# Gathers and sums of the routed experts as two lines of the planned order, six tiles of gathered rows, and a new test for shared chunks

## Chip, core and metric

One Trainium2 chip, one core. The metric is the device time of one execution in microseconds (us). The kernel before has a median of 2207.93 us in three runs (2204.1, 2207.93, 2208.98).

## What is computed

Input is x, two sequences of 2048 tokens with 256 features, all in float32. Four residual blocks follow one another:

```python
x = x + attention(layernorm(x))   # 16 heads, causal, weights scaled by a spectral norm
x = x + ffn(layernorm(x))         # f = 0: 8 experts, top 2 of them, plus a shared expert
x = x + gated(layernorm(x))       # x * softplus(x W1 + b1) * (x W2 + b2 . x W3 + b3)
x = x + ffn(layernorm(x))         # f = 1: same weights as f = 0
```

where ffn is

```python
scores = softmax(xt @ gate_w.T + gate_b); top_w, top_i = top_k(scores, 2)
out_e  = (silu(xt @ w1[e].T + b1[e]) * (xt @ w3[e].T + b3[e])) @ w2[e].T + b2[e]
y      = sum over the two picked experts of top_w * out_e
z      = (silu(xt @ ws1.T + bs1) * (xt @ ws3.T + bs3)) @ ws2.T + bs2
return y + z
```

## The kernel before, in words

The 4096 tokens are eight chunks of 512 (TC = 8), four to each of the two batches b; a chunk has four blocks of 128 tokens (NB = 4). X[c] holds a chunk in SBUF from start to end, and every stage adds to it in place.

The first half is the attention, with an order written out in a loop (L546 and after). The change touches only where three of its small tiles live: part (L318), nmt (L362) and rc (L425).

The second half, from about 1143 us, runs the two ffn blocks and the gated block. Its parts are Python generators. Each yield is a tuple of costs (DVE, ACT, PE, POOL) in us of what is issued next; a yield of None means "can't go on yet".

- route(f, c) (L736) normalizes a chunk, flips it to a feature-major tile xT and picks two experts for each token. sort(f, b) (L797) gives each token its slots in a list ordered by expert; weigh (L865) gives the gates. These three are the line routing.
- scatter(f, b) (L884) writes the normalized rows of a batch to the DRAM list XS[b] by 32 indirect DMAs from POOL, each followed by a small memset, and then marks (f, b) as placed.
- routed(f, b) (L1039) is the expert block, 39 blocks of 128 slots (EB): load rows of XS (SP queue), turn them (PE, ACT), up (PE; ea on DVE; Silu on ACT; es on DVE), turn, down (PE; ey on DVE), write to YS[b] (SP queue). When it is done, (f, b) is marked as ran.
- shared(f, c) (L1000) is the shared expert on one chunk: eight steps of the matmul s, then four of sy, 1.72 us of PE each. It reads the chunk's xT and frees it at the eighth step.
- combine(f, c) (L908) gathers, for each block, its two rows per token from YS[b] by two indirect DMAs from POOL into tiles yg (four of them), and adds them to X[c] by two DVE instructions (the sums, L933). For f = 1 it then issues the chunk's store to the output on SP.
- mixer(c) (L946) is the gated block on a chunk, after its combine: norm (with pow on POOL, L717), flip, z (PE, DVE), softplus through ACT, DVE and POOL (POOL lines L976, L986, L990), and the add to X[c] (L994).

moving() (L1156) is one line: scatter (0,0), scatter (0,1), then combine of the four f = 0 chunks of batch 0, scatter (1,0), combine of those of batch 1, scatter (1,1), and combine of all f = 1 chunks. mixing() is the line of the eight mixers, routing() the third. The three are in sides, in this order.

The planner writes the program. The main loop (L1214) takes steps of the expert block and of a shared chunk in turn ("mains"); free[2] is PE's planned time, called now here. After each step beside() (L1178) issues what fits from the sides: it goes through them in order, issues the first step that may go, and starts again. A step may go if each engine that it uses is planned free no later than now + LEAD (DVE 1.7, ACT 1.3, POOL 2.7), and its line's own time no later than now + AHEAD (DVE 1.5, ACT 1.5, POOL 2.7). A line's time is the planned end of its last step plus 0.2. A shared chunk is begun if its xT is there and either all three xT tiles are live (live[0] >= XTS), or no expert block is running or placed; the last condition is "not wait".

So the order on each engine is fixed when the program is built; on the chip only semaphores act. The names (0,1) and the like below are (f, b) for scatters and experts and (f, c) for shared chunks.

Of the kernel before, what the change touches and what calls it, by code (L numbers as in the profile page):

```python
# [8 lines left out]
F32 = mybir.dt.float32  # L9
# [7 lines left out]
P = 128  # L17
D = 256
# [26 lines left out]
KTE = 8  # L45
EARLY = 8
LOW = -3e38
LAG = 3


@with_exitstack
def hybrid_block(
# [87 lines left out]
    with tc.tile_pool(name="aw", bufs=1) as aw, ExitStack() as aw_ctx:  # L140
# [104 lines left out]
            yield 1  # L245

        with ExitStack() as ac:
            xnp = ac.enter_context(tc.tile_pool(name="xnp", bufs=1))
            xtp = ac.enter_context(tc.tile_pool(name="xtp", bufs=3))
            skp = ac.enter_context(tc.tile_pool(name="skp", bufs=2))  # L250
# [62 lines left out]
            class Maxima:  # L313


                def __init__(self, b, c, g):
                    self.unit, self.q = (b, c, g), qT[b, g, c]
                    self.part = small.tile(  # L318
                        [P, NB, 4, NCH], F32, tag="part", name=f"part_{b}_{g}_{c}"
                    )  # L320
                    self.full = [(kc, i) for kc in range(c) for i in range(NB)] + [(c, NB - 1)]
                    self.diag = [(c, i) for i in reversed(range(NB - 1))]
                    self.left = len(self.full) + len(self.diag)
# [33 lines left out]
            def shift(b, c, g, part, t):  # L357

                nc.vector.tensor_reduce(
                    t[:, :, 0:4], part[:, :, :, 0:c + 1], AX.X, ALU.max, negate=True  # L360
                )
                tt = small.tile([P, NB * 32], F32, tag="nmt", name=f"nmt_{b}_{g}_{c}", bufs=2)  # L362
                nc.vector.transpose(tt, t.rearrange("p n r -> p (n r)"))
                rows = qT[b, g, c][HD::32, :].rearrange("j (n a t) -> j n a t", a=4, t=32)
                for a in range(4):
                    nc.sync.dma_start(
                        rows[:, :, a, :],
                        tt[32 * a:32 * a + 4, :].rearrange("j (n t) -> j n t", t=32),
                    )
# [48 lines left out]
            def finish(b, c, g):  # L418

                ot = acc.pop((b, c, g))  # L420
                ps = bank(f"pso_{b}_{g}_{c}")
                for i in range(NB):
                    nc.tensor.transpose(ps[:, i * P:(i + 1) * P], ot[:, i * P:(i + 1) * P], ident)
                pv = ps.rearrange("p (m r) -> p m r", r=32)
                rc = small.tile([P, NB * 4], F32, tag="rc", name=f"rc_{b}_{g}_{c}")  # L425
                nc.vector.reciprocal(rc, pv[:, :, HD])
                if g == 0:
                    otok[b, c] = okp.tile([P, NB, NG, 4 * HD], F32, tag="otok", name=f"otok_{b}_{c}")
                nc.vector.tensor_tensor(
                    otok[b, c][:, :, g, :].rearrange("p n (j d) -> p n j d", d=HD),  # L430
                    pv[:, :, 0:HD].rearrange("p (n j) d -> p n j d", j=4),
                    rc.rearrange("p (n j) -> p n j", j=4).unsqueeze(3).to_broadcast([P, NB, 4, HD]),
                    ALU.mult,
                )
# [249 lines left out]

    scores, picks, sel, slots, gates, words = {}, {}, {}, {}, {}, {}
    xhat, xhatT = {}, {}
    live, held = [0], [0]

    added, mixed, sorted_, placed, joined, ran = set(), set(), set(), set(), set(), set()
# [2 lines left out]
    def feature_major(nm):  # L692
        while live[0] >= XTS:
            yield None
        live[0] += 1
        return cw.tile([P, 2, CH], F32, tag="xT", name=f"xT_{nm}", bufs=XTS)

    def token_major(nm):
# [37 lines left out]
    def route(f, c):  # L736

        b, q = divmod(c, NCH)
        nm = f"{f}_{c}"
        while f == 1 and c not in mixed:  # L740
            yield None
        if q == 0:
            scores[f, b] = rw.tile([P, BLK, E], F32, tag="lg", name=f"lg_{f}_{b}", bufs=1)
            picks[f, b] = rw.tile([P, TOPK, BLK, E], F32, tag="pick", name=f"pick_{f}_{b}", bufs=1)
            sel[f, b] = rw.tile([P, E, BLK], BF16, tag="sel", name=f"sel_{f}_{b}", bufs=1)
        blk = slice(q * NB, (q + 1) * NB)
        xn = yield from token_major(f"f{nm}")
        yield from normed(X[c], xn, f"f{nm}")
        xhat[f, c] = xn
        yield (0, 0, 0, 2.4)  # L750
        nc.gpsimd.tensor_tensor(
            X[c], X[c], bs2_s.unsqueeze(1).to_broadcast([P, NB, D]), ALU.add
        )
        xT = yield from feature_major(f"f{nm}")
        yield from flipped(xn, xT, f"f{nm}")
        xhatT[f, c] = xT
        yield (0.2, 0, 1.8, 0)
        ps = side_bank(f"psl_{nm}")
        for i in range(NB):
            for d in range(2):  # L760
                nc.tensor.matmul(  # L761
                    ps[:, i * E:(i + 1) * E], xT[:, d, i * P:(i + 1) * P], gw_s[:, d, :],
                    start=d == 0, stop=d == 1,
                )
        lg = scores[f, b][:, blk, :]
        nc.vector.tensor_tensor(
            lg, ps[:, :NB * E].rearrange("p (n e) -> p n e", e=E),
            gb_s.unsqueeze(1).to_broadcast([P, NB, E]), ALU.add,
        )
        yield (1.6, 0, 0, 0)  # L770

        ge = small.tile([P, NB, E, E], F32, tag="ge", name=f"ge_{nm}", bufs=2)
        nc.vector.tensor_tensor(
            ge, lg.unsqueeze(2).to_broadcast([P, NB, E, E]),
            lg.unsqueeze(3).to_broadcast([P, NB, E, E]), ALU.is_ge,
        )
        nc.vector.tensor_tensor(
            ge, ge, before.unsqueeze(1).to_broadcast([P, NB, E, E]), ALU.mult
        )
        up = small.tile([P, NB, E], F32, tag="rup", name=f"rup_{nm}", bufs=2)  # L780
        dn = small.tile([P, NB, E], F32, tag="rdn", name=f"rdn_{nm}", bufs=2)
        nc.vector.reduce_sum(up, ge, axis=AX.X)
        nc.vector.reduce_sum(dn, ge.rearrange("p n e j -> p n j e"), axis=AX.X)
        yield (0.6, 0, 0, 0)
        nc.vector.tensor_tensor(up, up, dn, ALU.subtract)
        pk = picks[f, b]
        for k in range(TOPK):
            nc.vector.tensor_tensor(
                pk[:, k, blk, :], up, level[:, k, :].unsqueeze(1).to_broadcast([P, NB, E]),
                ALU.is_equal,  # L790
            )
        nc.vector.tensor_tensor(
            sel[f, b][:, :, blk].rearrange("p e n -> p n e"), pk[:, 0, blk, :], pk[:, 1, blk, :],
            ALU.add,
        )
# [109 lines left out]
        yield (0, 0, 0, 0.5)  # L905
        placed.add((f, b))

    def combine(f, c):  # L908

        b, q = divmod(c, NCH)  # L910
        while (f, b) not in ran:
            yield None
        got = {}
        for i in range(NB + 1):
            if i < NB:
                n = q * NB + i
                for k in range(TOPK):
                    yield (0, 0, 0, 1.3)
                    y = ew.tile([P, D], F32, tag="yg", name=f"yg_{f}_{c}_{i}_{k}", bufs=4)
                    nc.gpsimd.indirect_dma_start(  # L920
                        out=y, out_offset=None, in_=YS[b],
                        in_offset=bass.IndirectOffsetOnAxis(
                            ap=slots[f, b][:, k, n:n + 1], axis=0
                        ),
                    )
                    got[i, k] = y
            elif q == NCH - 1:
                yield (0, 0, 0, 1.5)
            if i > 0:
                yield (1.0, 0, 0, 0)  # L930
                n = q * NB + i - 1
                for k in range(TOPK):
                    nc.vector.scalar_tensor_tensor(  # L933
                        X[c][:, i - 1, :], got.pop((i - 1, k)), gates[f, b][:, k, n:n + 1],
                        X[c][:, i - 1, :], ALU.mult, ALU.add,
                    )
        if f == 0:
            joined.add(c)
            return
        while (f, c) not in added:  # L940
            yield None
        nc.sync.dma_start(
            out[c * CH:(c + 1) * CH, :].rearrange("(n p) d -> p n d", p=P), X[c]
        )
# [211 lines left out]
    def moving():  # L1156
        yield from scatter(0, 0)
        yield from scatter(0, 1)
        for f, b in rows[:2]:
            for c in chunks(b):  # L1160
                yield from combine(f, c)
            yield from scatter(1, b)
        for c in range(TC):
            yield from combine(1, c)

    def mixing():
        for c in range(TC):
# [5 lines left out]
    LEAD = (1.7, 1.3, 0.0, 2.7)  # L1173
    AHEAD = (1.5, 1.5, 0.2, 2.7)

    sides = [[0.0, g, None] for g in (moving(), mixing(), routing())]

    def beside():  # L1178

# [34 lines left out]
    while sides or todo or shares or mains:  # L1214
        if "share" not in mains:
            fit = [s for s in shares if s in xhatT]
            wait = "experts" in mains or (todo and todo[0] in placed)
            if fit and (live[0] >= XTS or not wait):
                shares.remove(fit[0])
                mains["share"] = shared(*fit[0])  # L1220
        if "experts" not in mains and todo and todo[0] in placed:
# [88 lines left out]
```

## Time and profile before

| | us |
|---|---|
| median of the runs (three) | 2207.93 |
| lowest and highest | 2204.1, 2208.98 |
| the profiled execution | 2117.58 |
| its span, first to last instruction | 2115.8 |
| mean granted TensorE clock in it | 0.983 |
| PE busy | 2010.0 (95%) |
| DVE busy | 1386.0 (66%) |
| POOL busy | 870.5 (41%) |
| 128 gathers (L920) busy on POOL | 128.2 |
| 128 sums (L933) busy on DVE | 66.5 |

The profile is of one execution, whose own time lies 90 us below the median of the timed runs; all durations below are from it. PE is TensorE's matmuls, DVE VectorE, ACT ScalarE, POOL GpSimd, SP the queue that issues the direct DMAs. In a row of the order of time the columns are start, duration, engine, line, instruction, output and input with shape, count, and in brackets the idle time before it and what ended it. In the stage table each engine has its busy time and number of instructions, and PEclk is the granted TensorE clock.

Events of the second half, from the orders of time of PE and POOL: experts (0,0) end at 1424; gathers of the f = 0 chunks of batch 0 issue from 1427.2 to 1494.5; scatter (1,0) 1638.8 to 1679.7; gathers of batch 1's f = 0 chunks 1680.0 to 1751.1; scatter (1,1) 1890.4 to 1930.7; gathers of the f = 1 chunks of batch 0 1931.0 to 1998.9; experts (1,1) end at 2062.5; gathers of the f = 1 chunks of batch 1 2065.9 to 2108.6.

### The profile page before, as it was taken

The page shows a single profiled execution, that of the slowest core. Times are in us where ns is not written, and L with a number is a line of the kernel's source. Part 1 is how long each engine was busy: PE and PEld are TensorE (multiplying, and loading weights), DVE is VectorE, ACT ScalarE, POOL GpSimd, SP SyncE. Part 2 cuts the span into 40 slices and gives each one's busy share as a digit, 9 for nine tenths or more (in the row PEclk, how much of TensorE's full clock was granted, in tenths as well). Part 3 has the DMA queues.
Part 4 walks back from the last instruction along what each step waited for, and adds up shares of the span by engine and source line. Part 5 has one row for each costly group of instructions (what it writes and reads, how often), then busy time and mean ns, then how long its engine had stood idle before and what let it go on. Part 6 is the DMA issues. An engine that isn't in the chain of part 4 may idle for free.

```text
span 2115.8 us, 36162 instructions
## 1 busy us (share of the span) xinstructions
PE 2010.0 (95%) x11840; PEld 1087.9 (51%) x11840; DVE 1386.0 (66%) x3428; ACT 1075.5 (51%) x1566; POOL 870.5 (41%) x1153
## 2 busy tenths in 40 slices
PE   6999999999999999999998999999999999999993
PEld 3444444444445444444444666655656556655662
DVE  4777777787776777777851546446776378663643
ACT  1657577577776667767784122324433244431330
POOL 4334345254343343434454171605422753346305
PEclk8999999999999999999999999999999999999997
DMA  3212110000000000000002321423210332013523
GB/s 97 77 36 64 34 33 5 10 1 7 6 7 6 6 1 7 4 4 4 2 2 86 135 90 46 150 80 113 80 41 18 130 112 78 28 40 134 165 76 121
DMA packets 87604, 113.04 MB, mean 53 GB/s; under 512 B 16385, under 2 KB 75137, under 8 KB 87297
## 3 DMA queue, kind: packets, MB, share of 16 engines
q1 hardware_dynamic: 73488, 75.08, 11.1%
q0 software_dynamic: 12288, 33.57, 4.8%
q8 instruction: 101, 1.65, 0.3%
q10 hardware_dynamic: 1648, 2.10, 0.3%
q14 instruction: 79, 0.64, 0.1%
HBM read 54.59 MB, written 51.64 MB: 50 GB/s over the span
## 4 chain that ended last, share of the span: by engine, by line
PE 82%; DVE 7%; ACT 3%; issue 3%; POOL 3%; DMA 2%; DVEq 0%; SPq 0%; POOLq 0%; ACTq 0%
PE st L386 15%; PE o L405 13%; PE psm L341 13%; PE eu L1085 10%; PE s L1011 7%; PE ed L1109 5%; PE sy L1028 4%; PE psk L275 3%; PE tr L1070 3%; PE psz L961 1%; PE psj L454 1%; POOL xs L893 1%; PE psv L301 1%; DVE junk L350 1%; PE psl L761 1%
## 5 line engine op out<-in xcount | busy, mean ns | idle before, releaser
L390 ACT ACTIVATE pt<-st 128x1024 f32<-128x1024 f32 (+3 forms) x640 | 556.0, 895 | 176.1 <-PE psm L341 123.3
L341 PE MATMUL psm<-kT,qT 32*128 32x512 f32 (+3 forms) x2560 | 621.8, 565 | 10.7 <-DMA kT<-sk 4.4
L386 PE MATMUL st<-qT,kT 32*128 32x512 f32 (+3 forms) x2560 | 604.8, 553 | 1.3 <-ACT pt L390 1.3
L355 DVE TENSOR_REDUCE part<-psm 128x1 f32<-128x512 f32 x768 | 477.1, 681 | 117.1 <-PE psm L341 113.6
L416 POOL TENSOR_TENSOR oa<-oa,op 128x512 f32<-128x512 f32 (+3 forms) x288 | 313.8, 1090 | 450.5 <-ACT op L414 450.0
L386 PEld LDWEIGHTS st<-qT,kT 32*128 32x128 f32 x2560 | 264.4, 184 | 228.0 <-ACT pt L390 140.5
L341 PEld LDWEIGHTS psm<-kT,qT 32*128 32x128 f32 x2560 | 274.6, 184 | 76.0 <-issue 20.1
L350 DVE CUSTOM_DVE_ANT_0 junk<-psm,maskq 128x384 bf16<-128x384 f32 (+3 forms) x512 | 250.8, 490 | 94.8 <-PE psm L341 29.9
L405 PE MATMUL o<-pt,v 128*32 128x512 f32 (+3 forms) x2560 | 301.2, 541 | 11.2 <-DVE part L355 6.7
L1085 PE MATMUL eu<-we,turned 128*128 x560 | 263.7, 593 | 0.0
L1092 ACT ACTIVATE es<-ea 128x256 f32<-128x256 f32 x156 | 65.0, 417 | 353.9 <-DVE ea L1090 353.8
L1011 PE MATMUL s<-xT_f,ws 128*128 128x512 f32 x512 | 232.6, 598 | 0.0
L920 POOL DMA_INDIRECT yg<-ys,slot x128 | 128.2, 1001 | 233.2 <-issue 84.6
L414 ACT COPY op<-o 128x512 f32<-128x512 f32 (+3 forms) x288 | 148.6, 516 | 64.5 <-PE o L405 46.9
L1090 DVE TENSOR_TENSOR ea<-eu,be 128x512 f32<-128x512 f32 x156 | 107.4, 689 | 109.5 <-PE eu L1085 108.9
L1109 PE MATMUL ed<-we,turned 128*128 x624 | 162.7, 383 | 14.5 <-ACT turned L1075 14.5
L393 POOL TENSOR_SCALAR_AFFINE_SELECT pt<-pt 128x256 f32<-128x256 f32 x256 | 103.0, 409 | 176.9 <-ACT pt L390 173.0
L405 PEld LDWEIGHTS o<-pt,v 128*32 128x32 f32 x2560 | 52.2, 108 | 214.4 <-DVE part L355 124.4
L1109 PEld LDWEIGHTS ed<-we,turned 128*128 128x128 f32 x624 | 116.1, 190 | 88.0 <-issue 49.0
L893 POOL DMA_INDIRECT xs<-xn_f,slot x128 | 124.9, 975 | 86.3 <-DVE slot L847 59.3
L1011 PEld LDWEIGHTS s<-xT_f,ws 128*128 128x128 f32 x512 | 95.3, 192 | 102.7 <-issue 96.4
L1085 PEld LDWEIGHTS eu<-we,turned 128*128 128x128 f32 x560 | 97.6, 190 | 75.1 <-issue 72.9
(268 smaller groups left out, 2099.4 us busy)
## 6 DMA issues: line engine op xcount, KB each, us to landing
xs<-xs SPq DMA_DIRECT2D x156, 128.0 KB
ys<-ey SPq DMA_DIRECT2D x156, 128.0 KB
xs<-zeros SPq DMA_DIRECT2D x78, 128.0 KB
we<-in_we_dram SPq DMA_DIRECT2D x8, 768.0 KB
kT<-sk SPq DMA_DIRECT2D x128, 32.0 KB
out_dram<-x SPq DMA_DIRECT2D x8, 512.0 KB
x<-in_x_dram SPq DMA_DIRECT2D x6, 512.0 KB
be<-in_be_dram SPq DMA_DIRECT2D x1, 3072.0 KB
```

What stands on the lines that cost most here:

```text
L341: nc.tensor.matmul(ps[:, :n], self.q[r, i * P:(i + 1) * P], kT[b, g, kc][r, :n], start=True, stop=True,)
L350: nc.vector.tensor_tensor_reduce(junk[:, :n], ps[:, :n], maskq[:, CH - n:], 1.0, LOW, ALU.add, ALU.max, m,)
L355: nc.vector.reduce_max(m, ps[:, :n], axis=AX.X)
L386: nc.tensor.matmul(st[:, i, off:], k[r, ks], q[r, off:], start=True, stop=True)
L390: nc.scalar.activation(pt[:, :, off:], st[:, :, off:], AF.Exp)
L405: nc.tensor.matmul(o[32 * j:32 * j + 32, off:], V[kb // NB][:, kb % NB, 4 * g + j, :], pts[j // 2][:, j % 2, off:], start=True, stop=True,)
L414: nc.scalar.copy(t[:, off:], o[:, off:])
L416: nc.gpsimd.tensor_tensor(a[:, off:], a[:, off:], t[:, off:], ALU.add)
L893: ins = nc.gpsimd.indirect_dma_start(out=XS[b], out_offset=bass.IndirectOffsetOnAxis(ap=slots[f, b][:, k, n:n + 1], axis=0), in_=xhat[f, b ...
L1011: nc.tensor.matmul(ps, w[:, d, cs], xT[:, d, :], start=d == 0, stop=d == 1)
L1085: nc.tensor.matmul(ps, t[:, 1, d * P:(d + 1) * P], we_s[:, bass.ds(v + d * CH, CH)], start=d == 0, stop=d == 1,)
L1109: nc.tensor.matmul(ps[:, 0:D], t[:, 0, d * P:(d + 1) * P], we_s[:, bass.ds(v + 2 * CH + d * D, D)], start=d == 0, stop=d == 1,)
```

## The change

combine is split. gather(f, c) issues the indirect DMAs and puts each block's pair of tiles into a list, landing, of at most GB = 3 blocks; yg has six tiles. combine(f, c) issues the sums, and may place those of a block once the next block's gathers have been issued (counted in sent). moving() now holds the scatters and gathers; a new line combining(), second in sides, holds the sums and stores. A count, turns, holds how many feature-major tiles are still to be asked for (24 in all: 8 by mixers, 16 by routes); the rule for shared chunks "all three xT tiles are live" is now "all three are live and more are to come". To make room, part, nmt and rc of the attention move from the pool small, which stays, to a pool asm that is released with the attention, and the tile ge of route has one buffer, not two.

```diff
+GB = 3
...
+            asm = ac.enter_context(tc.tile_pool(name="asm", bufs=3))
...
-        ge = small.tile([P, NB, E, E], F32, tag="ge", name=f"ge_{nm}", bufs=2)
+        ge = small.tile([P, NB, E, E], F32, tag="ge", name=f"ge_{nm}", bufs=1)
...
+    turns = [TC + 2 * TC]
...
         live[0] += 1
+        turns[0] -= 1
...
-    def combine(f, c):
+    landing = []
+    sent = [0]
+
+    def gather(f, c):
 
         b, q = divmod(c, NCH)
         while (f, b) not in ran:
             yield None
...
+        for i in range(NB):
+            n = q * NB + i
+            rows = []
+            for k in range(TOPK):
+                while len(landing) == GB:
+                    yield None
+                yield (0, 0, 0, 1.3)
+                y = ew.tile([P, D], F32, tag="yg", name=f"yg_{f}_{c}_{i}_{k}", bufs=2 * GB)
+                nc.gpsimd.indirect_dma_start(
...
+                rows.append(y)
+            landing.append(rows)
+            sent[0] += 1
+        if q == NCH - 1:
+            yield (0, 0, 0, 1.5)
+            sent[0] += 1
+
+    def combine(f, c):
+
+        b, q = divmod(c, NCH)
+        for i in range(NB):
+
+            at = (f * TC + c) * NB + i + f * B + b + 2
+            while sent[0] < at:
+                yield None
+            yield (1.0, 0, 0, 0)
+            n = q * NB + i
+            for k, y in enumerate(landing.pop(0)):
+                nc.vector.scalar_tensor_tensor(
+                    X[c][:, i, :], y, gates[f, b][:, k, n:n + 1], X[c][:, i, :],
+                    ALU.mult, ALU.add,
+                )
...
             for c in chunks(b):
-                yield from combine(f, c)
+                yield from gather(f, c)
             yield from scatter(1, b)
         for c in range(TC):
-            yield from combine(1, c)
+            yield from gather(1, c)
+
+    def combining():
+        for f in range(2):
+            for c in range(TC):
+                yield from combine(f, c)
...
-    sides = [[0.0, g, None] for g in (moving(), mixing(), routing())]
+    sides = [[0.0, g, None] for g in (moving(), combining(), mixing(), routing())]
...
-            if fit and (live[0] >= XTS or not wait):
+            if fit and (live[0] >= XTS and turns[0] or not wait):
```

More of the change, by code (lines that the diff above doesn't have):

```diff
@@ L317, in __init__ @@
                     self.unit, self.q = (b, c, g), qT[b, g, c]
-                    self.part = small.tile(
+                    self.part = asm.tile(
                         [P, NB, 4, NCH], F32, tag="part", name=f"part_{b}_{g}_{c}"
@@ L361, in shift @@
                 )
-                tt = small.tile([P, NB * 32], F32, tag="nmt", name=f"nmt_{b}_{g}_{c}", bufs=2)
+                tt = asm.tile([P, NB * 32], F32, tag="nmt", name=f"nmt_{b}_{g}_{c}", bufs=2)
                 nc.vector.transpose(tt, t.rearrange("p n r -> p (n r)"))
@@ L424, in finish @@
                 pv = ps.rearrange("p (m r) -> p m r", r=32)
-                rc = small.tile([P, NB * 4], F32, tag="rc", name=f"rc_{b}_{g}_{c}")
+                rc = asm.tile([P, NB * 4], F32, tag="rc", name=f"rc_{b}_{g}_{c}")
                 nc.vector.reciprocal(rc, pv[:, :, HD])
@@ L912, in combine @@
             yield None
[L913 to L936, printed above, removed]
+        for i in range(NB):
[7 more added lines that the diff above has]
+                nc.gpsimd.indirect_dma_start(
+                    out=y, out_offset=None, in_=YS[b],
+                    in_offset=bass.IndirectOffsetOnAxis(
+                        ap=slots[f, b][:, k, n:n + 1], axis=0
+                    ),
+                )
[17 more added lines that the diff above has]
+                    ALU.mult, ALU.add,
+                )
         if f == 0:
```

## The prediction

> **What bounds the kernel now.** I read the 40 slices first, then the busy times of the last stages, then POOL and PE in order of time, the view of the gathered tile, and the waits.
>
> ```profile
> ## 2 busy tenths in 40 slices
> PE   6999999999999999999998999999999999999993
> ...
> POOL 4334345254343343434454171605422753346305
> ```
>
> PE is full nearly to the end of both halves. The second half starts near 1143 us; what is left of PE's idle time lies in the last slice. The stages show how the end is made:
>
> ```profile
> core 0: us, PE busy (x) PEld busy (x) DVE busy (x) ACT busy (x) POOL busy (x), PEclk, DMA share, GB/s
> ...
> 1950.00:2000.00 50.00, 50.00 (x200) 31.63 (x199) 32.93 (x71) 16.62 (x34) 22.69 (x23) 1.00 0.58 176
> 2000.00:2050.00 50.00, 50.00 (x200) 31.54 (x199) 25.68 (x54) 16.93 (x34) 0.00 (x0) 1.00 0.31 98
> 2050.00:2116.00 66.00, 31.80 (x109) 19.23 (x108) 25.05 (x50) 6.07 (x12) 30.89 (x32) 0.77 0.35 108
> ```
>
> From 2000 to 2050 POOL does nothing: the 32 gathers of the last four chunks need the last expert block. PE in order of time, around that block's end:
>
> ```profile
> 2061.57 1.13 PE L1109 MATMUL ed<-we,turned 128*128 x4 [0.52 <-ACT turned L1075]
> 2062.54 13.90 PE L1011 MATMUL s<-xT_f,ws 128*128 128x512 f32 x32
> 2076.28 7.07 PE L1028 MATMUL sy<-ws,hsh 128*128 128x256 f32 x32
> ```
>
> After it one shared chunk runs, 2062.5 to 2083.4 (20.8 us), and PE is done. POOL gathers from 2065.94 to 2109.6 and the span ends at 2115.8. So the end is the last expert block's end (2062.5) plus 53.3 us, and only one of 16 shared chunks lies in that tail, which has room for more than two. **The end falls if PE reaches 2062.5 earlier: by less idle time before it, or by a whole shared chunk moved behind it.**
>
> PE between experts (1,0) and (1,1):
>
> ```profile
> 1915.03 1.03 PE L1109 MATMUL ed<-we,turned 128*128 x4
> 1915.90 13.90 PE L1011 MATMUL s<-xT_f,ws 128*128 128x512 f32 x32
> 1929.63 1.89 PE L1028 MATMUL sy<-ws,hsh 128*128 128x256 f32 x8
> 1934.29 0.41 PE L1070 MATMUL tr_-4_17532<-ident,xs 128*128 128x128 f32 x2 [2.77 <-DMA xs<-xs]
> ```
>
> When the planner saw (1,1) placed, shared chunk (1,6) had done its eight first steps (13.9 us) and stood before its last four. A chunk once started is interleaved with the experts and ends before them. So a placing earlier by less than about 13 us moves no chunk; by 13 to 34 us it moves one, 20.8 us.
>
> What sets the placing is a chain: gathers and sums, four mixers, routes, sort, scatter. The pow (L717) of mixers 0 to 3 marks its pace:
>
> ```profile
> 1448.82 1.05 POOL L717 TENSOR_TENSOR lnrs_b<-lnve_b,nhalf 128x4 f32<-128x4 f32 x1 [1.53 <-DVE lnve_b L715]
> 1505.97 1.16 POOL L717 TENSOR_TENSOR lnrs_b<-lnve_b,nhalf 128x4 f32<-128x4 f32 x1 [10.54 <-DVE lnve_b L715]
> ...
> 1544.97 1.14 POOL L717 TENSOR_TENSOR lnrs_b<-lnve_b,nhalf 128x4 f32<-128x4 f32 x1 [7.44 <-DVE lnve_b L715]
> ...
> 1581.68 1.04 POOL L717 TENSOR_TENSOR lnrs_b<-lnve_b,nhalf 128x4 f32<-128x4 f32 x1 [6.78 <-DVE lnve_b L715]
> ```
>
> 57, 39, 37 us: the mixer beside the gathers is 19 us slower than its fellows. In batch 1 POOL's order of time gives 54, 42, 38 (1699.9, 1753.9, 1795.9, 1834.0): 16 us. So 35 us is the most that a faster gather stage can give to the chain.
>
> **Two lines instead of one.** By the planner's costs a block is now 2 x (1.3 + 0.2) + 1.0 + 0.2 = 4.2 us, 16 blocks 67 us; the trace agrees (first to last gather issue 1427.2 to 1494.5). Split, the gather line takes 3.0, the sums follow at the same pace: 48 us. On the chip a gather takes 1.25 us (tail), so POOL can follow. Six tiles let it run three blocks ahead. In the tile's view, "who waited for it", POOL stands 74.3 us for its tiles:
>
> ```profile
> L920 POOL DMA_INDIRECT yg<-ys,slot x128: 942/952/1942, 1427.2 to 2108.6; - x128
> ...
>   POOL yg L920: 74.3, 43
>   DVE x L933: 17.4, 21
> ```
>
> None of the 74.3 is worth its size: except in the tail, only what hastens the mixers counts. Nothing but order moves: the same 128 gathers, 128 sums and 8 stores. The gathers move past the mixers' elementwise work on POOL; the stores past nothing on SP that is waited for.
>
> What the split costs: the gather line stands first and refills POOL to its lead of 2.7 us; a mixer's POOL step (pow, L976, L986, L990) then fits only where that lead lies in the last 0.2 us before the next gather. Following the costs by hand from the end of experts (0,0), chunk 0 is joined about 2 us sooner, the pow comes about 12 us later than now (34 after the start, not 22), but the gathers end near 1475, nothing stands before L976 and after, and mixer 0 ends near 1493 instead of 1498.9. Mixer 1's statistics, now held to 1502.8 by the last sums, then start near 1494: 9 us gained. Bounds: 19 (all of the slowdown), and -12 (the pow shut out until 1475, then the 35 us that a free mixer needs from there, 1510). In batch 1 the phase is kinder to the pow; mixer 4 ends 2 us earlier, and the 6 us that sums take from mixer 5 (statistics to flip 8 us, against 4 for mixer 2) go: 8 us, bounds 16 and -14. Sum 17 us, between -26 and 35. I take 17, nearest to the trace's shape, in which the stage ends with its gathers. 17 is beyond 13, so chunk (1,6) goes to the tail.
>
> **Sums earlier in DVE's order.** A sum is placed once the next block's gathers are in the program, no longer when they are planned to end, so DVE, which is in order, may stand before it for data; behind it wait ea, es and ey, and PE waits for those through turned. Landing takes 2.7 to 2.8 us from issue; at the starts of the two stages PE itself waits for xs, so I take 0 to 1.5 us there. DVE's own load rises: per block of 3.02 us, ea 0.69, es 0.42 and ey 0.42, plus 0.99 of sums, 2.5 us or 83%, and the mixer's norm on top. Now PE idles 0 us in 1430 to 1500 and 4 us in 1720 to 1750. I add 3 us, bounds 0 and 10.
>
> The rule that speaks against this: the Trainium skill, SBUF — State Buffer, Who interferes with whom, says that a VectorE instruction with two SBUF inputs contends with a GpSimd one that reads SBUF, and that one blocks fully. A sum has two, yg and x. If gathers counted as such, packing sums beside them could hold each of 64 blocks up to 0.95 us, some 30 us in the two inner stages, on an engine at 83%. The row: in the tail, beside back-to-back gathers, the sums take 0.48 us, as elsewhere; beside L990 one took 3.1 us. So the rule holds for the mixers' POOL work, not for gathers; the split parts sums from that work, and I add nothing.
>
> **Tail.** Twelve gathers from 2065.94 took 18.8 us where 12 x 1.25 is 15.0: 3.8 us lost to sums queued behind the shared chunk's DVE steps. With three blocks of lead this goes when one chunk is in the tail. With two (41.6 us), sums paced at 3.0 hold the gathers part of the way: I give 2.3 of the 3.8 back.
>
> **Shared chunks kept.** The new test matters only while three feature-major tiles are live and none is to come: after the last flip (about 1875) it holds (1,5) back from 1888 until experts (1,0) end. PE then does the same work in another order; the gap before the placing takes (1,5) anyway. 0 us, hidden by that gap; only if the placing came 34 us earlier would it keep three. A little more DVE load in the last sort is at most 2 us of the 17.
>
> **asm, ge.** The first half's three small tiles go to a pool that is released; same instructions. ge with one buffer is written and read by DVE alone: nothing waits. A shift of addresses could change which late tile the first loads wait for: 0, bounds -2 and 3.
>
> **Sum.** 2115.8 - 20.8 (chunk moved) - 1.5 (tail) + 3 (DVE) = 2096.5, that is -19. The profiled execution took 2117.58, the median of the runs is 2207.93, 90 us more; no row shows where, and the saving is of program order, so I carry it over: 2189.
>
> **Rivals.**
> - Chain faster, but by less than 13 us: no chunk moves. -3.8 + 2 to 3: about -1.5, 2206. For it: 17 stands only 4 above the threshold, and jitter of a planner step is 1.7. Against: both stages point the same way.
> - Starved mixers, slower: if the pow is shut out in both stages the placing is late by over 6.9 us, the four steps (1,6) has left, and (1,7) is started before it. Then nothing is left for the tail: +20.8 - 3.8 + 1 = +18, 2226. The point is the phase of the gather line: lead above 2.7 after each step. Against it: the lead drifts by 0.02 us per block and opens the window within about ten blocks.
> - DVE as the bound of the two stages: +10 instead of +3 and no chunk: +6, 2214.
> - The placing comes 34 us early: two chunks more, -40, 2168.
>
> **Chances.** One chunk moved 0.53; none, small gain 0.24; slower by starving or DVE 0.20; two chunks 0.03. A difference of 0.2% (4.4 us) is about what a measurement of this kernel can tell from none. Faster: 0.53 + 0.03 and 0.01 of the second case, 0.57; same 0.23; slower 0.20. The range runs from 2178 (one chunk with the idle time saved too) to 2222, which takes in the unmoved case and most of the slower ones.
>
> **What would show it.** Right: gathers of (0,0) to (0,3) issued within 50 us; L717 of mixers 0 and 1 under 50 us apart; the last expert block near 2044 with 64 matmuls of s behind it, 32 now; "POOL yg" waiting for x under 30 us. Wrong: 32 or none behind it; sums with a long wait for yg inside an expert block; PE waiting for turned by over 10 us more than the 13.2 now.

## The result, and the profile after

After takes 2227.5 us (2222.7 to 2230.2, five runs), before 2207.4 (2201.2 to 2209.0) on the same chip: ratio 1.0096, 95% interval 1.0083 to 1.0109. That is 20 us slower, where 19 us faster was forecast.

One thing must be known to read the rest. The runs were made in six sets, each on one chip, and the sets fall into two kinds: in four of them before took 2199 to 2207 us, in two 2119 to 2120. The profile that the prediction was read from (2117.6 us) is of the second kind, the timed runs shown with it (2207.9) are of the first. I call the chips *disturbed* and *quiet*; one chip was met in two sets, both times disturbed, so that it is the chip and not the hour is likely but not shown. Every ratio below is against before on the same chip. Times of two disturbed chips are set beside each other only for after and for the runs of before again, the new test alone and the four tiles, where before took 2207.4 and 2206.9.

The order came out as forecast. PE in order of time at the end of after (disturbed chip):

```profile
2169.82 1.13 PE L1128 MATMUL ed<-we,turned 128*128 x4 [0.52 <-ACT turned L1094]
2170.78 13.90 PE L1030 MATMUL s<-xT_f,ws 128*128 128x512 f32 x32
2184.52 7.07 PE L1047 MATMUL sy<-ws,hsh 128*128 128x256 f32 x32
2191.42 13.90 PE L1030 MATMUL s<-xT_f,ws 128*128 128x512 f32 x32
```

Two shared chunks stand behind the last expert block, where before had one. But that block ends at 2170.8, not near 2044. The 40 slices of after's page show where the time went:

```profile
PE   7999999999999999999989895979996899958997
...
POOL 4434345254344443344442624034336243353205
```

The first line is PE, the second POOL, in tenths. PE is no longer full in the second half. The stretches with 5 to 8 tenths are those in which POOL scatters or gathers. Who was held, in the waits of after (total us, times, longest):

```profile
PE ed L1128 <- ACT turned L1094: 53.7, 28, 17.0
ACT turned L1094 <- remote: 49.7, 8, 13.7
DVE ea L1109 <- remote: 43.3, 5, 15.2
ACT hsh L1032 <- remote: 29.2, 3, 21.0
DVE hsh L1035 <- remote: 20.6, 1, 20.6
DVE x L1053 <- remote: 16.9, 2, 9.1
DVE ey L1134 <- remote: 14.4, 4, 9.1
```

"Remote" is a release that the view can't name. 174 us of such waits stand here, and 9 on POOL's own memset; the profile of before that the prediction was read from has none. All six groups are instructions of ACT and DVE that take a result of TensorE out of PSUM, the memory it writes to; the sums, the statistics and the products in SBUF are not among them.

The trace itself says more than the view. In it 3191 TensorE instructions count up one semaphore, for which ACT and DVE wait. All 23 of these waits of ACT and DVE ended when this semaphore, which no other engine counts up, was updated, and that update came 1.5 to 16.3 us after the end of TensorE's last matmul that counts it up. The nine waits of POOL ended on its own semaphore, updated 1.6 to 2.7 us after its last memset. So what came late is the signal, or the end of a matmul, which the profile only models; the trace can't tell these apart.

### The profile page after: what moved, and what is told of

It reads as the page before. It is cut to its first block, busy times and chain, and to the rows that moved or that the text cites. A ratio compares the mean times of both kernels' runs of the same rounds, so it can differ in the third digit from the quotient of the medians.

```text
span 2228.2 us, 36158 instructions
## 1 busy us (share of the span) xinstructions
PE 2041.7 (92%) x11840; PEld 1101.6 (49%) x11840; DVE 1383.4 (62%) x3428; ACT 1073.3 (48%) x1566; POOL 865.7 (39%) x1153
## 4 chain that ended last, share of the span: by engine, by line
PE 75%; DVE 8%; another core or an unknown queue 5%; ACT 5%; issue 4%; POOL 1%; DMA 1%; DVEq 0%; SPq 0%; POOLq 0%; ACTq 0%
PE st L388 14%; PE o L407 12%; PE psm L343 12%; PE eu L1104 9%; PE s L1030 7%; PE ed L1128 5%; PE sy L1047 3%; PE psk L277 3%; PE tr L1089 2%; PE psj L456 1%; PE psz L980 1%; DVE junk L352 1%; PE psv L303 1%; PE psl L765 1%
## 5 line engine op out<-in xcount | busy, mean ns | idle before, releaser
L1104 PE MATMUL eu<-we,turned 128*128 x560 | 272.6, 610 | 0.0
L1030 PE MATMUL s<-xT_f,ws 128*128 128x512 f32 x512 | 239.2, 611 | 17.9 <-DVE hsh L1035 8.4
L1128 PE MATMUL ed<-we,turned 128*128 x624 | 171.6, 399 | 82.7 <-ACT turned L1094 53.7
L1094 ACT COPY turned<-tr 128x512 f32<-128x512 f32 (+1 forms) x156 | 87.4, 560 | 126.7 <-PE tr L1089 62.8
```

The lines of the kernel that those rows point to most:

```text
L1030: nc.tensor.matmul(ps, w[:, d, cs], xT[:, d, :], start=d == 0, stop=d == 1)
L1104: nc.tensor.matmul(ps, t[:, 1, d * P:(d + 1) * P], we_s[:, bass.ds(v + d * CH, CH)], start=d == 0, stop=d == 1,)
L1128: nc.tensor.matmul(ps[:, 0:D], t[:, 0, d * P:(d + 1) * P], we_s[:, bass.ds(v + 2 * CH + d * D, D)], start=d == 0, stop=d == 1,)
```

## The experiments

**How lost TensorE time is counted.** Where PE's idle time is too coarse (a matmul after a stall is slow too), I weigh every matmul by its start-to-start time in the quiet profile of before: 0.43 us for s and eu, 0.22 for sy and ed, 0.24 for psz, 0.11 for flips and tr. A stretch's length less this sum is its loss, good to about 4 us, since some records are missing and the ends of a stretch can be set a little differently.

### Is the profile of before an ordinary one?

The kernel before, unchanged:

> The kernel before, unchanged, profiled once more. Theory A (the profiled execution that the prediction was read from, 2117.6 us, was an unusual one; an ordinary one holds about 90 us of TensorE idle time in the second half, most of it in the four stretches in which GpSimd scatters the sorted rows): the span is 2200 to 2210, and the new PE idle time sums to 80 to 100 us, with at least two thirds of it inside the four scatter stretches. Theory B (the stalls seen after belong to the changed order): the span is near 2116 again, PE is over 99% busy from 1200 to 1300, and the timed 2207 stays unexplained.

It took 2207.2 us (ratio 0.9995, 0.9984 to 1.0005), its span is 2205.7. PE and the granted TensorE clock in 40 slices, then PE and DVE in order of time, beside the second scatter (1331 to 1375):

```profile
PE   7999999999999999999989895999998699987993
...
PEclk9999999999999999999999997999999899998997
```

```profile
1345.36 1.89 PE L1028 MATMUL sy<-ws,hsh 128*128 128x256 f32 x8
1361.68 2.04 PE L1109 MATMUL ed<-we,turned 128*128 x4 [14.43 <-DVE x L1034]
...
1364.37 3.22 PE L1085 MATMUL eu<-we,turned 128*128 x4
1378.05 2.07 PE L1109 MATMUL ed<-we,turned 128*128 x4 [10.46 <-DVE ey L1115]
```

```profile
1360.84 0.69 DVE L1034 TENSOR_TENSOR x<-x,sy 128x512 f32<-128x512 f32 x1 [19.38 <-remote]
1361.45 0.42 DVE L1098 TENSOR_TENSOR es<-es,ea 128x256 f32<-128x256 f32 x1
1376.38 0.69 DVE L1090 TENSOR_TENSOR ea<-eu,be 128x512 f32<-128x512 f32 x1 [14.52 <-remote]
```

PE ends its sy at 1347.2, and DVE, with nothing else to do, takes the result at 1360.8. PE ends its eu at 1367.6, and DVE takes it at 1376.4, just after the last scatter (1374.7). Meanwhile PE stands, for these very instructions of DVE and their followers (14.43 and 10.46 us). After a stall it is slow: from 1361 to 1390 the granted clock is 0.66, and four ed take 2.04 us, 1.03 elsewhere. So theory A holds: the four scatters lose 9, 28, 22 and 23 us here, and the 75 us that PE idles more than in the quiet profile (97 against 22, gaps over 1.5 us; 80 to 100 expected) and the slow matmuls after each stall make up the 90 us that the prediction had "no row" for. Before is held too, by 160 us of remote waits. A lower clock all along is not the reason: PE starts the second half at 1153.5 in both profiles, and they part only with the scatters. What after adds to it is still open.

### The parts of the change

Before with these lines alone (e2), and after without the last of them (e3):

```diff
+    turns = [TC + 2 * TC]
+        turns[0] -= 1
-            if fit and (live[0] >= XTS or not wait):
+            if fit and (live[0] >= XTS and turns[0] or not wait):
```

> Before with the new test for shared chunks alone. In the program's order it only takes chunk (1,5) from beside experts (1,0) into the gap before experts (1,1). Prediction's step (0 us): within 4 us of before, 2204 to 2212. Rival (the experts left alone beside the fourth scatter have nothing to fill their waits): slower by 10 us or more, 2217 to 2230, with the new idle time of PE between 1900 and 2010.

> After without the new test: two lines and six tiles alone. In the program's order chunk (1,5) runs beside experts (1,0), no chunk stands in the gap before experts (1,1), and (1,6) and (1,7) lie in the tail. Theory A with the loss in the two lines: 2220 to 2235, PE idle in the gap for the fourth scatter's end, about as after. Rival (the test for the chunks is what costs): 2190 to 2207.

e2: 2213.1 us beside 2206.9, ratio 1.0033 (1.0022 to 1.0044), 6 us slower; between the two forecasts. The fourth scatter loses 25.9 us where before lost 22.7, and the stretch from its end to the last experts 8.0 instead of 5.0. With chunk (1,5) gone from beside it, PE waits more; each of the two differences is within the error of the count, together they are the 6 us. e3: 2230.4, ratio 1.0111 (1.0083 to 1.0138). So the test isn't what costs; the two lines with their six tiles are. e3 again, beside after, on another disturbed chip:

> Two lines and six tiles without the new test for the shared chunks (2230.4 where before took 2206.9). The prediction gave the test 0 us. Where before takes 2119: within 3 us of after if that holds; 5 to 20 us slower than after if the chunk that the test keeps for the gap before the last experts fills idle time there. Where before takes 2206: 2226 to 2234.

It took 2222.8 us, and after 2222.0 on that chip: with the two lines the test is worth nothing there.

### The lead of the gathers

After with four tiles in place of six, PE's order unchanged:

```diff
-GB = 3
+GB = 2
```

> After with four tiles of gathered rows in place of six (two blocks of lead, not three); PE's order in the program is the same. If the lead of the gathers matters (more of their transfers beside the experts' loads), 5 us or more faster than after, 2215 to 2222; if only the order matters, within 4 us of after, 2224 to 2232; if the lead is what helps the tail, 2230 to 2240.

2217.2 us, ratio 1.0045 (1.0029 to 1.0061), 10 us less than after's 2227.5. The first gather stage shows why. In after, PE stood 6.4 us there, for ACT and DVE that were let go together:

```profile
1478.01 0.42 DVE L1117 TENSOR_TENSOR es<-es,ea 128x256 f32<-128x256 f32 x1
1484.21 0.69 DVE L1109 TENSOR_TENSOR ea<-eu,be 128x512 f32<-128x512 f32 x1 [5.78 <-remote]
...
1484.20 0.58 ACT L1094 COPY turned<-tr 128x512 f32<-128x512 f32 x1 [6.57 <-remote]
...
1484.84 2.07 PE L1128 MATMUL ed<-we,turned 128*128 x4 [6.41 <-ACT turned L1094]
```

With six tiles the first dozen gathers go out back to back, like a scatter; before's gathers, and those of the four tiles, wait for a tile after four. Remote waits beside gathers are in after at 1484, 1769, 1799 and 2059; before again and the four tiles have none. The lead is a part of it only: the four tiles are still 10 us slower than before.

### Is it GpSimd's indirect DMA?

Before, and then after, with the scatters as plain DMAs (the rows reach the wrong experts, so the output is not the reference's):

```diff
-                    ins = nc.gpsimd.indirect_dma_start(out=XS[b], out_offset=..., in_=xhat...)
+                    m = k * CH * NCH + n * P
+                    ins = nc.sync.dma_start(out=XS[b][m:m + P, :], in_=xhat...)
```

> Before, with the 128 scatters of rows by index replaced by 128 plain DMAs of the same 128 rows each from SyncE, to rows in running order, so the rows reach the wrong experts and the output is not the reference's; bytes and order of the work are the same. If the scatters by GpSimd are what holds the other engines up in an ordinary execution: 2115 to 2140, near the one unusual profile of before. If the DMA traffic itself does it, whatever its queue: 2195 to 2215.

> After, with the scatters as plain DMAs in running order (the rows reach the wrong experts, the output is not the reference's), beside 2112.1 of before with the same edit. If the prediction's sum holds wherever the scatters don't disturb (-20.8 for the chunk, the rest small): 2091 to 2097. If the gathers' two lines lose TensorE time of their own (13 to 26 us in three stages, read off after) and the tail is 3.6 longer: 2106 to 2122.

On a disturbed chip before with plain scatters takes 2112.1 us beside 2205.4: ratio 0.9569 (0.9549 to 0.9590), and no remote wait is left. PE in its slices:

```profile
PE   7999999999999999999998999999999999999993
```

So the 93 us hang on the scatters by GpSimd; the same bytes from SyncE hold nothing up. The edit changes the queue and the order of the rows in DRAM at once; which of the two counts was not tested apart. The Trainium skill's page "DMA: Bandwidth & Descriptors", section "SWDGE vs HWDGE vs iDMA", also keeps DMAs from SyncE out of the path in SBUF through which GpSimd's DMAs go; but the harm that it tells of is GpSimd locked out by VectorE, and here VectorE and ScalarE are the ones that wait. After with plain scatters took 2093.6 on a quiet chip, beside 2119.2 of before; on a disturbed one it was not run.

### Does the rate matter?

The scatter has a memset between two steps. Before with three wider ones (e5; a step of 2.2 us, not 1.26), after with two memsets behind each gather (e6, the last two lines), and both in after (e8):

```diff
-    between = fw.tile([1, 1], F32, tag="between", name="between")
+    between = fw.tile([1, 256], F32, tag="between", name="between")
-                    nc.gpsimd.memset(between, 0.0)
+                    for _ in range(3):
+                        nc.gpsimd.memset(between, 0.0)
...
+                for _ in range(2):
+                    nc.gpsimd.memset(between, 0.0)
```

(e5 also gives ge one buffer, to make room.)

> Before, with 0.93 us of GpSimd memsets between two steps of the scatter in place of 0.09, so that a step takes about 2.2 us and not 1.26; the order of all other engines is the same. Weighing each TensorE instruction by its undisturbed time, the four scatters of the repeated profile of before hold 9, 28, 22 and 23 us of lost TensorE time, and gathers at 2.1 us a step none. Theory R (it is the rate of indirect DMAs that holds the other engines up): under 8 us lost in each scatter, 55 to 65 us less in all; a scatter ends 28 us later, of which 10 to 25 come back as idle time before the experts that need it: 2150 to 2175. Rival D (every indirect DMA costs the others a fixed time): the loss stays, and the later ends come on top: 2210 to 2240.

> After, with two memsets (0.6 us) behind each gather, so that a gather step takes 1.9 us and not 1.25; the order of the other engines is the same as in after. Theory R: the 26 us that the three gather stages of after lose more than those of before shrink to under 12, the tail grows by 3 to 8 us: 2208 to 2222. Rival D: no gain, the tail longer: 2228 to 2240.

> After with both spacings (0.93 us in the scatters, two or three memsets behind each gather). Theory R: both gains, less the idle time before the experts and the longer tail: 2145 to 2180, and the chunk in the tail now shows its worth, so below the version of before with spaced scatters. Rival D: 2235 to 2260.

e5: 2200.9 us, ratio 0.9972 (0.9959 to 0.9985), where 2150 to 2175 was expected. No remote wait is left, but the gain is eaten by what I had put at 10 to 25 us. PE, before the third and the fourth expert block:

```profile
1740.09 0.66 PE L1071 MATMUL tr_-4_15850<-ident,xs 128*128 128x128 f32 x2 [30.47 <-DMA xs<-xs]
...
2020.29 0.66 PE L1071 MATMUL tr_-4_17788<-ident,xs 128*128 128x128 f32 x2 [30.31 <-DMA xs<-xs]
```

The scatters take 24 to 28 us longer, and PE, no longer held, comes early. In the first scatter PE also stands 5.8 and 14.0 us, since VectorE waits for a pow of GpSimd that comes late in the longer train. e6 took 2214.2, ratio 1.0032 (1.0019 to 1.0045), inside its forecast, but not for the reason forecast: I had overlooked that the wider tile lengthens the scatter's own memset to 0.30 us (a step of 1.43). The remote waits fell to 51 us, all beside scatters, which lost about 3, 20, 9 and 23 us. (The expectation of e9 below has 12 for the last; by the trace it is 23, with PE idle for 15.9 us of it.) The gather stages have no remote wait left but lose 14, 11 and 10 us still, in part waiting for results of the mixers, whose GpSimd work now stands among the memsets. And the tail grew to 73 us. e8 took 2243.0, ratio 1.0164 (1.0137 to 1.0190): no remote wait, but both idle gaps (29 and 28 us) and the long tail; my 2145 to 2180 was wrong since it put these too low.

So the scatter's spacer alone, at 0.30 us, in before (e9) and in after (e10):

```diff
-    between = fw.tile([1, 1], F32, tag="between", name="between")
+    between = fw.tile([1, 256], F32, tag="between", name="between")
```

> Before, with only the scatter's spacer grown from 0.09 to 0.30 us (a step of 1.43 us in place of 1.26). The run with spaced gathers had this spacer too, and its scatters lost 3, 22, 9 and 12 us where those of after lost 9, 31, 22 and 30; so its 13 us may be the scatters' and not the gathers'. Theory S (the loss hangs on the scatter's rate): 30 to 40 us less lost in before too, 2168 to 2185. If the gain came from the gathers' spacing: 2200 to 2210.

> After, with only the scatter's spacer grown to 0.30 us, the gathers as in after. Theory S: 45 us less lost than after in the scatters, and the tail is after's 57 us, not 73: 2178 to 2195. If the spacing of the gathers was what helped: 2222 to 2230.

and a version put together from it, after with four tiles and 0.93 us in the second scatter:

```diff
-GB = 3
+GB = 2
-                    nc.gpsimd.memset(between, 0.0)
+                    for _ in range(3 if (f, b) == (0, 1) else 1):
+                        nc.gpsimd.memset(between, 0.0)
```

> After with four tiles, the scatter's spacer at 0.30 us, and 0.93 us in the scatter of batch 1 in the first half of the expert layers, for which nothing waits for long. Theory S with the four tiles' 10 us: 2217 less 45 less another 20 in the second scatter: 2150 to 2165, faster than both kernels. If the spacing only puts the loss elsewhere: 2190 to 2215.

These three ran on a quiet chip, which the expectations had not reckoned with. There e9 is slower (2133.2 beside 2119.2, ratio 1.0067, 1.0048 to 1.0087): PE waits 7.6 and 8.5 us for xs before the last two blocks, 2.1 and 2.8 before. e10 took 2106.7 (ratio 0.9936, 0.9920 to 0.9953), e12 2112.8 (0.9974, 0.9964 to 0.9983). The paced version again, with after, on a disturbed chip:

> The kernel after, unchanged. Two kinds of chips have shown themselves: on two of them before takes 2205 to 2207 us, on a third 2119. Theory C (the sign of the change hangs on whether the scatters disturb the other engines on the chip): where before takes about 2119, after takes 2098 to 2108, faster by 0.5% to 1%; where before takes about 2206, 2222 to 2230 again. Rival (after loses by its own order, whatever the chip): slower than before by about 20 us on either.

> After with four tiles and the slower scatters (0.30 us of spacer, 0.93 in the second scatter), which took 2112.8 where before took 2119.2. Theory S: where before takes about 2206, the scatters lose 45 to 65 us less than after's: 2145 to 2175. Rival (the pacing moves the loss): 2195 to 2215. Where before takes 2119: 2111 to 2115 again.

After: 2222.0 us beside 2199.1, ratio 1.0106 (1.0089 to 1.0123). Paced: 2130.9, ratio 0.9682 (0.9659 to 0.9704), better than the 2145 to 2175 expected. So it is faster than both kernels on a disturbed chip; on a quiet one it beats before (2112.8 beside 2119.2) but not after (2095.2 beside 2119.6, next section). PE in its slices:

```profile
PE   6999999999999999999998999999999899998997
```

PE is nearly full again, and no remote wait is left. One thing doesn't fit: e6 had the same 1.43 us step in its third and fourth scatter and still lost 9 and 23 us there, with remote waits; the paced version lost 6 and 6, without. So rate matters, but it isn't all. Which part of the paced version's edit does it isn't shown: the 1.43 us step alone met only quiet chips.

### Is the predicted gain there on a quiet chip?

> The kernel after, unchanged. Where before takes about 2119: theory C 2098 to 2108; if after loses by its own order, 2130 to 2140. Where before takes 2200 to 2207: 2220 to 2228 a third time.

> Before with the scatter's spacer at 0.30 us (a step of 1.43 us), which took 2133.2 where before itself took 2119.2. Where before takes about 2203: by theory S the disturbance of the scatters falls by most of its 90 us, as in the paced kernel (2130.9 beside 2199.1): 2130 to 2150. If the paced kernel's gain came from its four tiles or its second scatter alone: 2180 to 2205. Where before takes 2119: 2133 again.

> After with the scatter's spacer at 0.30 us, six tiles, which took 2106.7 where before took 2119.2 and before with the same spacer 2133.2 (26 us apart). Where before takes about 2203: theory C (without the disturbance the predicted gain is there) 15 to 27 us faster than before with the same spacer, 2105 to 2130. If the two lines lose time of their own there: within 5 us of it, or slower.

These ran on a second quiet chip. After, unchanged: **2095.2 us beside 2119.6, ratio 0.9878 (0.9861 to 0.9896)**, faster by 24 us, where 2098 to 2108 was expected; its span is 2095.3, where the prediction's sum for the profiled execution was 2096.5. With the 1.43 us scatter before takes 2137.6 (1.0086, 1.0069 to 1.0103) and after 2107.0 (0.9945, 0.9932 to 0.9957). So the two lines lose nothing of their own there. PE of after on the quiet chip, in its slices and at the end:

```profile
PE   6999999999999999999998999999999999999998
```

```profile
2043.83 1.13 PE L1128 MATMUL ed<-we,turned 128*128 x4 [0.52 <-ACT turned L1094]
2044.80 13.90 PE L1030 MATMUL s<-xT_f,ws 128*128 128x512 f32 x32
```

Where the sign turns, by stretch (lost TensorE time, us; the first four columns on disturbed chips):

| stretch | before again | after | four tiles | paced | after, quiet |
|---|---|---|---|---|---|
| scatter (0,1) | 28 | 31 | 27 | 2 | -2 |
| gathers (0, batch 0) | -2 | 13 | 4 | 4 | -1 |
| scatter (1,0) | 22 | 22 | 23 | 6 | 1 |
| gathers (0, batch 1) | 3 | 8 | 6 | 5 | 3 |
| scatter (1,1) | 23 | 30 | 31 | 6 | -2 |
| gathers (1, batch 0) | -3 | 6 | 5 | 5 | 1 |

The scatter (0,0) loses 9 us in before again and in after alike. Between the first two columns lie 39 us, by this count 29 of them in the gather stages. (From 1150 us to the end of the last expert block the count, which no choice of stretches touches, gives 163.7 and 203.4, 40 us.) With the chunk moved (-20.8) and a tail of 57.2 us, not 53.6 (+3.6), that makes +22; the two profiles are 22.5 apart (2228.2 and 2205.7). Of the 40 us the tiles' lead is shown by experiment, for 10 us; the rest is placed by the profiles, not taken apart.

## Why the prediction was wrong

- **The end and the chunk: right, the sum in part by luck.** On the quiet chip the last expert block ends at 2045.0 (forecast near 2044) with 64 matmuls of s behind it. That is 17.5 us earlier, with 20.8 us of work moved; the other 3.3 us look like the +3 of the sum but are not VectorE's. PE idles 3.4 us less than before up to there, and what it loses more lies mostly in two stretches of low granted clock: 0.65 from 1676 to 1684 and 0.51 from 1842 to 1849. The chunk came from another place than I argued: it left the gap before experts (1,0), which I had not looked at. Before ran 28 matmuls of s there at 1669.1; after on the quiet chip runs none between its last ed (1670.9) and the first tr (1675.1).
- **Two lines: right in kind, 12 us for 17.** On the quiet chip the gathers of batch 0 are issued in 43 us (forecast 48, before 67), mixer 1's statistics start at 1493.8 (forecast near 1494, before 1502.8), and the pow of mixers 0 and 1 stand 42 us apart (57):

```profile
1454.81 1.04 POOL L721 TENSOR_TENSOR lnrs_b<-lnve_b,nhalf 128x4 f32<-128x4 f32 x1
1496.87 1.05 POOL L721 TENSOR_TENSOR lnrs_b<-lnve_b,nhalf 128x4 f32<-128x4 f32 x1 [5.48 <-DVE lnve_b L719]
```

  The pow of mixer 0 came 27 us after the start of its stage, not 34: it was not shut out as long as the following of the costs by hand had it. From the start of a gather stage to the next scatter it is 200 us in place of 212, and 204 in place of 210: 12 and 6, for 9 and 8; the second start came only 5 us earlier, so (1,1) is scattered 11 to 12 us earlier, not 17. That is under my threshold of 13, and the chunk moved all the same: the threshold, read off one gap of the trace, was not the planner's.
- **Sums earlier, +3 us: 0 on the quiet chip** (PE waits 13.5 us for turned; before it is 14.5, not the 13.2 of the prediction). The rule that I weighed and set aside stays aside: a sum there takes 0.48 us in the median and 0.55 at most. In the profile of after on a disturbed chip PE waits 53.7 us for turned, as the prediction's sign of being wrong had it ("over 10 us more"), but for results of TensorE that ACT and DVE get late, not for sums in DVE's order; in that of after again it is 20.0.
- **Tail: right.** 50.3 us on the quiet chip (51.8 forecast). On the disturbed one 57.2: one x of the shared chunk was held 7.7 us there.
- **The test for shared chunks, 0 us: right in after's order, not alone.** Its cover was the gap, but beside the fourth scatter chunk (1,5) had been cover for PE on a disturbed chip: 6 us.
- **asm, ge:** not run by themselves.
- **The step that failed** is the sentence "no row shows where, and the saving is of program order, so I carry it over". The profiled execution, 90 us below the median of the runs, was of another regime. The 90 us were PE's, lost beside scatters of GpSimd (with plain DMAs in their place before takes 2112.1). The change makes GpSimd's other indirect DMAs, the gathers, denser, and on a disturbed chip PE then loses 40 us more before the end of the experts, against 20.8 us moved behind it: 20 us slower in place of 19 faster. There the sentence "None of the 74.3 is worth its size" was false too: POOL's waits for its tiles kept the gathers apart, and with four tiles 10 of the 20 us went.
- **Rivals:** "starved mixers" gave 2226, nearly the time measured, for a reason that didn't happen: one chunk did move to the tail, and on the quiet chip the mixers gained.

What stays open is how a scatter by GpSimd makes TensorE's signal late, and what makes a chip quiet. Instruction loads don't tell it: after and before again have the same 101 and 78 packets in their two queues. The traces hold one more trait of the disturbed chips. There, fewer updates of the semaphores of PE, DVE, ACT and POOL are recorded than instructions that make them: 276 fewer in before again, 322 in after, nearly all in the stretches in which GpSimd issues indirect DMAs, gathers too. On quiet chips none are missing, nor in the profile that the prediction was read from. With plain scatters on a disturbed chip 120 are missing, all beside gathers, though no time is lost there. So the trait goes with the chip and with indirect DMAs, and not with the scatters' loss alone; whether counts are merged on their way or only their records are lost, and whether the recording itself takes part in the delay, these runs don't show.

## What to carry to other kernels

If the profiled execution is not as long as the runs, find that difference first: a forecast from such a profile holds for other conditions, and a change can have the other sign there. A wait on an engine off the critical path may be what spares the critical one, so ask what the engine will do at full rate before you remove it. Try pacing long trains of indirect DMAs, and weigh it on both kinds of chip: 0.2 us more between two scatters (0.9 in one of the four) and one block less of lead took 91 us off after where it was held up. Where nothing is held it costs: there it still beat before by 6 us, but the slower scatter alone made before 14 to 18 us slower and after 12.

## What the hardware showed that I had not expected

On the disturbed chips a train of 32 scatters at 1.26 us a step left ACT and DVE waiting up to 21 us at a time for results of TensorE, and in before again and after TensorE lost 22 to 31 us in each train of about 45 us but the first (9); at 2.2 us a step no such wait was left, and with plain DMAs of the same rows from SyncE neither (2112.1 beside 2205.4). On the quiet chips the same program ran at 2119 to 2120 with the trains at 1.26 us. ACT and DVE were often let go within 0.1 us of each other (1484.20 and 1484.21 in after; 1267.40 and 1267.34 in before again).
